# A graph-attention layer and an 8-head attention layer: the fourth pair's product between its scores, the projection and statistics one stretch sooner, the norms later

## The chip, the cores and the metric

The kernel runs on one core of a Trainium2 chip. The metric is the device time of one execution in microseconds (us). Five engines work side by side, each through its own queue in order: TensorE (PE, with PEld for its weight loads), VectorE (DVE), ScalarE (ACT), GpSimd (POOL) and SyncE (SP, which here only issues transfers). Each of them waits for the others through semaphores.

## The reference

The input x has 32 batch entries of 512 nodes with 512 features, and one adjacency matrix of 512 x 512 serves them all. Layer 0 is a graph attention whose output goes beside its own projection; layer 1 is an 8-head attention with heads of 64. Each layer is added to its input and normalised.

```python
# layer 0, per batch entry: W is 512 x 256, a is 2 x 256
h = X @ W
e = leaky_relu(h @ a[0] + (h @ a[1]).T, 0.2) - 1e9 * (1 - adj)
x = layernorm(X + concatenate([softmax(e) @ h, h], axis=-1))
# layer 1, per batch entry and head
q, k, v = (split_heads(x @ W.T + b) for W, b in ((Wq, bq), (Wk, bk), (Wv, bv)))
s = where(adj == 0, -inf, q @ k.T / 8)
x = layernorm(x + merge_heads(softmax(s) @ v) @ Wo.T + bo)
```

All arithmetic is in 32-bit floats.

## The kernel before

A batch entry (below: a batch) is four tiles of 128 nodes. The loop goes over the 32 batches, and in each over four pairs of heads, hp = 0 to 3 (first to fourth pair). Batches 1 to 29 are written by `middle_batch`; the first and the last two by the general loop behind it, with the same steps in a slightly different order. The program is not reordered by any scheduler: each engine executes its instructions in the order in which the Python code emits them. So a step that stands earlier in the code stands earlier in the queue of every engine that it uses, and an instruction that waits holds up all that follows on its engine.

The work of three batches is interleaved. While layer 1's attention of batch b runs, layer 0 of batches b+1 and b+2 and the output projection of batch b-1 fill the gaps. The steps that matter here:

- `head_scores(b, hp, i)` makes the scores of tile i for both heads of a pair on TensorE (L701, into PSUM tiles ps, of which there are four). VectorE adds the mask and takes the row's minimum of the negated scores (L315), and ScalarE takes exponentials (L710) into a tile p.
- `head_blocks` transposes four such tiles p in blocks of 32 x 32 on VectorE into one buffer t (L330). It is called twice a pair, after tiles 0 and 1 and, from `pair_ends`, after tiles 2 and 3.
- `head_move` moves t to the buffer pt by 16 transfers on SP's queue (L347), which finishes the transpose. There is one buffer t and one buffer pt: the next pair's blocks wait until t has been moved away, and the next move waits until pt has been used.
- `head_products` multiplies pt by the values on TensorE (L763, pav), for the pair before the current one (`last`). `head_divide` multiplies the result by the inverse sums on VectorE (L778).
- `project_two(b, s)` makes queries and keys of two pairs with seven products in place of eight (L547, PSUM tiles pw). Three products go to three PSUM banks; ScalarE copies each out (L571: p1, p5, p7, later u2), and the next product adds into the first bank, so that it has to wait for the copy p1. VectorE adds the pieces (L584). `next(two)` runs it up to and with u2.
- `finish_seven(b - 1)` is the output projection of the batch before (L802, pf), with additions to the residual x on VectorE and GpSimd (L825).
- `out_stats(b - 1)` takes mean and variance of the four finished tiles on VectorE (L280, L281); `ln_root` takes the square root on ScalarE (L286), which needs another table of functions than the exponential; `out_norm` takes the reciprocal and shift on VectorE (L291, L911) and normalises on ScalarE (L915); `store` writes the batch out.
- `l0_project(b + 2, i)` is layer 0's projection (L264, ph; copied by ScalarE in L369), `l0_columns` sends the attention terms through DRAM on SP's queue (L387 to L391), `l0_maxima`, `l0_write` and `l0_read` make the row maxima from them (L404, L315, L421, L426).

PSUM tiles of tag m (pav, pf, ph, pw and others) take turns in four banks, in the order of the code. Tiles p, the copies of `project_two` and those of `l0_maxima` take turns in nine buffers.

Of the kernel before, what the change touches and what calls it, by code (L numbers as in the profile page):

```python
# [26 lines left out]
def kernel(  # L27
# [48 lines left out]
    B, N, F = x.shape  # L76
# [3 lines left out]
    NB = N // P  # L80
# [202 lines left out]
    def ln_root(key, tiles=range(NB)):  # L283
        mv, rstd = st["ln", key]
        lo, hi = tiles[0], tiles[-1] + 1
        nc.scalar.activation(rstd[:, lo:hi], mv[:, lo:hi, 1], AF.Sqrt, bias=eps)  # L286
# [84 lines left out]
    def l0_project(b, i):  # L371

        l0_copy(b, i, l0_product(b, i))
# [526 lines left out]
    def out_stats(b):  # L900
        z, key = st["x1", b], f"1_{b}"
        for i in range(NB):
            ln_stats(z, key, i)
# [28 lines left out]
    def steps(todo):  # L932
        for _ in todo:
            pass
# [37 lines left out]
    two = project_two(0, 0)  # L972
# [29 lines left out]
    def middle_batch(b):  # L1002


        seven = finish_seven(b - 1, lambda: load_x(b + 1, nc.gpsimd))
        for hp in range(NP):
            last = (b, hp - 1) if hp > 0 else (b - 1, NP - 1)
            head_scores(b, hp, 0)
            head_scores(b, hp, 1)
            if hp in (1, 2):  # L1010
                head_products(*last)
            if hp == 0:
                values = project_v(b)
                next(values)
                l0_scores(b + 1, [0, 1])
            elif hp == 1:
                next(seven)
                l0_add_h(b + 1)
            elif hp == 2:
                add_bias(b + 1)  # L1020
            head_blocks(b, hp)
            if hp == 3:
                out_stats(b - 1)
                for i in range(NB):
                    l0_project(b + 2, i)
                l0_columns(b + 2)
                ln_root(f"1_{b - 1}")
            head_scores(b, hp, 2)
            head_scores(b, hp, 3)
            if hp == 2:  # L1030
                next(seven)
            else:
                if hp == 3:
                    out_norm(b - 1)
                if hp != 1:
                    head_products(*last)
            pair_ends(b, hp)
            if hp == 2:
                next(seven)
            head_divide(*last)  # L1040
            if hp == 0:
                l0_row(b + 1)
                l0_scores(b + 1, [2, 3])
                leaky(st["row", b + 1])
                next(values)
                l0_weights(b + 1)
                head_inverse(b, 0)
                steps(values)
                next(seven)
                next(seven)  # L1050
            elif hp == 1:
                l0_output(b + 1)
                load_xt(b + 2)
                two = project_two(b, 1)
                next(two)
                l0_norm(b + 1)
                next(two)
                head_inverse(b, 1)
                blocks = x1_blocks(b + 1)
                for part in (blocks, two, blocks, two, blocks):  # L1060
                    next(part, None)
            elif hp == 2:
                steps(seven)
                x1_sums(b + 1, nc.gpsimd)
                head_inverse(b, 2)
                if b == 1:
                    add_bias(1)
            else:
                l0_maxima(b + 2)
                l0_write(b + 2)  # L1070
                l0_read(b + 2)
                store(b - 1)
                steps(project_two(b + 1, 0))
                head_inverse(b, 3)

    before = None
# [1 line left out]
    for b in range(B):  # L1078
        if 0 < b < B - 2:
            middle_batch(b)  # L1080
            before = (b, NP - 1)
            continue
        more = b < B - 1
        seven = finish_seven(b - 1) if b > 0 else None
        for hp in range(NP):

            head_scores(b, hp, 0)
            head_scores(b, hp, 1)  # L1090
            if hp == 0:
                values = project_v(b)
                next(values)
                if more:
                    l0_scores(b + 1, [0, 1])
            elif hp == 1:
                if b == 0:
                    l0_output(1)
                else:
                    if more:  # L1100
                        l0_weights(b + 1)
                        l0_add_h(b + 1)
                    next(seven)
            elif hp == 2:
                if b > 0:
                    next(seven)
                if b > 0 and more:
                    add_bias(b + 1)
            else:
                if b > 0:  # L1110
                    if b + 2 >= B:
                        steps(seven)
                    if not more:
                        output_weights()
                    out_stats(b - 1)
                else:
                    weight_sums(OUTPUT, nc.gpsimd)
                    add_bias(0)
                if b + 2 < B:
                    for i in range(NB):  # L1120
                        l0_project(b + 2, i)
                    l0_columns(b + 2)
                if b > 0 and b + 2 < B:
                    ln_root(f"1_{b - 1}")
            head_scores(b, hp, 2)
            head_scores(b, hp, 3)
            if b > 0 and hp in (1, 2):
                next(seven)
            if b > 0 and hp == 3 and b + 2 < B:
                out_norm(b - 1)  # L1130
            if (b, hp) not in turned:
                head_blocks(b, hp)
                head_reciprocal(b, hp)
                head_sums(b, hp)
                head_move(b, hp)
            if hp == 0 and b > 0 and more:
                load_x(b + 1)
            if before is not None:
                head_values(*before)
            if (b, hp) == (B - 1, 3):  # L1140
                last_products(b, 0)
                last_products(b, 1)
            if (b, hp) in turned:
                head_turn(b, hp)
            if hp == 0:
                if more:
                    l0_row(b + 1)
                    leaky(st["row", b + 1])
                next(values)
                head_inverse(b, 0)  # L1150
                if more:
                    l0_scores(b + 1, [2, 3])
                steps(values)
                if b == 0:
                    l0_weights(1)
            elif hp == 1:
                head_inverse(b, 1)
                if b > 0 and more:
                    next(seven)
                    l0_output(b + 1)  # L1160
                if b + 2 < B:
                    load_xt(b + 2)
                two = project_two(b, 1)
                next(two)
                if more:
                    l0_norm(b + 1)
                next(two)
                blocks = x1_blocks(b + 1) if more else None
                for part in (blocks, two, blocks, two, blocks):
                    if part:  # L1170
                        next(part, None)
                if not more:
                    next(seven)
            elif hp == 2:
                if b == 0:
                    output_bias()
                else:
                    next(seven)
                    if b + 2 < B:
                        steps(seven)  # L1180
                head_inverse(b, 2)
                if more:
                    x1_sums(b + 1, nc.gpsimd)
            else:
                if b + 2 < B:
                    l0_maxima(b + 2)
                    l0_write(b + 2)
                    l0_read(b + 2)
                if b > 0 and b + 2 < B:
                    store(b - 1)  # L1190
                if more:
                    two = project_two(b + 1, 0)
                    next(two)
                    if b + 2 >= B:
                        ln_root(f"1_{b - 1}")
                        out_norm(b - 1)
                        store(b - 1)
                    steps(two)
                head_inverse(b, 3)
                if b == 0:  # L1200
                    weight_negative(OUTPUT)
            before = (b, hp)
    b = B - 1
# [73 lines left out]
```

## Time and profile before

| what | value |
|---|---|
| runs before | 3148.51, 3152.12, 3158.78 us; median 3152.12 us |
| the profiled execution's own time | 3155.16 us |
| its span, first to last instruction | 3153.4 us |
| mean granted TensorE clock | 0.993 |
| TensorE, matmuls busy | 3062.0 us (97%) |
| VectorE busy | 2551.2 us (81%) |
| ScalarE busy | 1535.9 us (49%) |
| GpSimd busy | 1286.3 us (41%) |
| scores L701 on TensorE | 2048 matmuls, 510.0 us |
| product with the values L763 | 2048 matmuls, 469.2 us |
| layer 0's projection L264 | 1024 matmuls, 234.9 us |
| statistics L280 on VectorE | 252, 170.7 us, 677 ns each |
| moves pt<-t on SP's queue | 1984 transfers of 128 KB, 2.4 us each to landing |

How to read it: the busy time of an engine is a sum over the whole span, and neighbouring matmuls overlap, so that 97% does not say that TensorE works at its peak. In the lists of groups the idle time before a group stands beside what ended it. A timeline row has the start in us from the span's start, the time that the row takes, the engine, the line, the operation, the tile written and read, and in square brackets the idle time just before it with the instruction that ended it. One batch takes about 96 us, so a row at 1474.14 lies in the middle of the run, in the fourth pair of a middle batch.

### The profile page before, as it was taken

How to read it: one execution, taken by the hardware profiler on the slowest of the kernel's cores; microseconds unless marked ns; L12 is line 12 of the kernel's file. 1: busy time of each engine (PE TensorE's matmuls, PEld its weight loads, DVE VectorE, ACT ScalarE, POOL GpSimd, SP SyncE). 2: the span in 40 equal slices, each digit the busy share in tenths (PEclk: the TensorE clock that was granted, in tenths of full speed). 3: DMA queues.
4: the chain of work that ended last, by engine and by line, in shares of the span. 5: the costliest groups of instructions: out<-in, count | busy, mean ns of one | idle time of the engine just before them, and what ended most of it. 6: DMA issues, size and time to landing. Idle time of an engine off the chain costs nothing.

```text
span 3153.4 us, 44630 instructions
## 1 busy us (share of the span) xinstructions
PE 3062.0 (97%) x13492; PEld 2072.1 (66%) x13492; DVE 2551.2 (81%) x5707; ACT 1535.9 (49%) x3264; POOL 1286.3 (41%) x1253
## 2 busy tenths in 40 slices
PE   8999999999999999999999999999999999999998
PEld 6666666666666666666666666666666666666665
DVE  7788888788788887888887878888888888788765
ACT  4444455445454444554455544555444555445544
POOL 4354343343434434434434334344344443343421
PEclk9999999999999999999999999999999999999999
DMA  6466656566566666666665656665666656566632
GB/s 185 107 147 160 149 141 160 144 151 152 146 151 143 152 156 146 155 146 145 163 152 141 156 142 154 153 155 146 150 144 164 151 144 159 140 156 151 152 94 64
DMA packets 237440, 462.53 MB, mean 147 GB/s; under 512 B 94544, under 2 KB 97104, under 8 KB 237200
## 3 DMA queue, kind: packets, MB, share of 16 engines
q1 hardware_dynamic: 216848, 395.42, 53.0%
q0 software_dynamic: 20352, 64.25, 6.5%
q8 instruction: 109, 1.79, 0.3%
q14 instruction: 131, 1.07, 0.1%
HBM read 132.65 MB, written 34.27 MB: 53 GB/s over the span
## 4 chain that ended last, share of the span: by engine, by line
PE 66%; DVE 13%; ACT 6%; SPq 6%; issue 4%; DMA 3%; POOL 2%; DVEq 0%; ACTq 0%; POOLq 0%
PE pw L547 18%; PE pv L623 12%; PE ps L701 10%; PE pav L763 9%; PE pf L802 8%; PE po L477 7%; SPq L347 6%; DVE t L330 5%; DVE stats L280 2%; ACT p L710 2%; DVE p L315 2%; ACT x L915 2%; DMA d_tot<-tot 1%; DMA xt<-in_xt_dram 1%; PE ph L264 1%
## 5 line engine op out<-in xcount | busy, mean ns | idle before, releaser
L710 ACT ACTIVATE p<-p,least 128x512 f32<-128x512 f32 x1024 | 726.4, 711 | 681.0 <-DVE least L315 673.5
L330 DVE STREAM_TRANSPOSE t<-p 128x512 f32<-128x512 f32 x992 | 636.3, 686 | 127.1 <-DMA d_tot<-tot 81.0
L315 DVE CUSTOM_DVE_ANT_0 p<-ps,mask 128x512 f32<-128x512 f32 x1024 | 642.0, 682 | 60.7 <-PE ps L701 60.6
L701 PE MATMUL ps<-qk 64*128 64x512 f32 x2048 | 510.0, 615 | 0.3 <-DVE least L315 0.3
L763 PE MATMUL pav<-pt,v 128*64 128x512 f32 x2048 | 469.2, 600 | 2.8 <-DMA pt<-t 2.8
L754 POOL DMA_DIRECT2D inv<-d_tot x256 | 134.1, 528 | 717.0 <-DVE least L315 241.5
L763 PEld LDWEIGHTS pav<-pt,v 128*64 128x64 f32 x2048 | 136.1, 137 | 320.2 <-issue 293.7
L701 PEld LDWEIGHTS ps<-qk 64*128 64x128 f32 x2048 | 177.0, 186 | 235.1 <-issue 153.0
L600 POOL TENSOR_TENSOR p<-p,p 128x512 f32<-128x512 f32 x64 | 83.7, 1308 | 436.0 <-ACT p L571 436.0
L825 POOL TENSOR_TENSOR x<-x,u_o 128x512 f32<-128x512 f32 x93 | 115.6, 1270 | 340.2 <-ACT u_o L820 340.2
L825 DVE TENSOR_TENSOR x<-x,pf 128x512 f32<-128x512 f32 x186 | 125.4, 677 | 150.9 <-POOL x L825 90.8
L477 PE MATMUL po<-h,et 128*128 128x257 f32 x1024 | 236.3, 388 | 2.8 <-ACT et L470 2.2
L264 PE MATMUL ph<-w_sb,xt 128*128 128x258 f32 x1024 | 234.9, 387 | 0.3 <-DVE w_sb L190 0.3
L477 PEld LDWEIGHTS po<-h,et 128*128 128x128 f32 x1024 | 190.6, 191 | 59.7 <-issue 14.2
L264 PEld LDWEIGHTS ph<-w_sb,xt 128*128 128x128 f32 x1024 | 193.3, 191 | 51.3 <-PE ps L701 22.0
L459 POOL TENSOR_TENSOR et<-et,mask0t 128x512 f32<-128x512 f32 x126 | 157.4, 1262 | 121.6 <-ACT et L455 121.5
L547 PE MATMUL pw<-tx,wqx_sb 128*128 128x256 f32 x512 | 138.2, 393 | 68.6 <-ACT p L571 68.6
L710 ACT ACTIVATION_READ_ACCUMULATOR p<-p,least 128x1 f32 x1024 | 192.1, 188 | 0.0
L280 DVE BATCH_NORM_STATS2 stats<-x 128x6 f32<-128x512 f32 x252 | 170.7, 677 | 17.9 <-POOL x L825 4.8
L710 ACT ACT_TABLE_LOAD x62 | 79.5, 1283 | 209.9 <-DVE least L315 209.4
L802 PE MATMUL pf<-wo_sb,ot 128*128 128x256 f32 x744 | 179.4, 384 | 0.0
L286 ACT ACTIVATE rstd<-mv,eps 128x4 f32<-128x4 f32 (+1 forms) x66 | 19.6, 297 | 324.8 <-DVE mv L281 321.7
(155 smaller groups left out, 5608.1 us busy)
## 6 DMA issues: line engine op xcount, KB each, us to landing
pt<-t SPq DMA_DIRECT2D x1984, 128.0 KB, 2.4
inv<-d_tot POOLq DMA_DIRECT2D x256, 128.0 KB, 3.4
xt<-in_xt_dram SPq DMA_DIRECT2D x31, 1024.0 KB, 7.4
x1t<-x1t_b SPq DMA_DIRECT2D x496, 64.0 KB, 2.0
out_dram<-x SPq DMA_DIRECT2D x31, 1024.0 KB, 7.1
x<-in_x_dram POOLq DMA_DIRECT2D x29, 1024.0 KB, 5.6
rows<-d_att SPq DMA_DIRECT2D x31, 512.0 KB, 3.8
rows<-d_least SPq DMA_DIRECT2D x31, 256.0 KB, 4.3
```

The source lines that it names most:

```text
L264: nc.tensor.matmul(ps, lhs(c), rhs(c), start=(c == 0), stop=(c == FC - 1))
L280: nc.vector.bn_stats(stats, z[:, i, :])
L315: nc.vector.tensor_tensor_reduce(out=out, in0=scores, in1=mask, scale=-1.0, scalar=MIN_INIT, op0=ALU.add, op1=ALU.min, accum_out=least,)
L330: nc.vector.transpose(t[:, :, :, i, :].rearrange("p r c q -> p c r q"), src.rearrange("p (c r k) -> p c r k", r=4, k=G),)
L477: nc.tensor.matmul(po, et[:, j, i * P : (i + 1) * P], h_sb[:, j, 2:], start=(j == 0), stop=(j == NB - 1),)
L547: nc.tensor.matmul(ps[:, k * half : (k + 1) * half], weights(k, c), moving(c), start=start and k == 0 and c == 0, stop=c == FC // 2 - 1, s ...
L623: nc.tensor.matmul(ps[:, k * half : (k + 1) * half], columns(k, c), weights(c), start=start and k == 0 and c == 0, stop=c == FC // 2 - 1, ...
L701: nc.tensor.matmul(ps, qk[rows, 0, i * P : (i + 1) * P], qk[rows, 1, :], start=True, stop=True)
L710: nc.scalar.activation(p, p, AF.Exp, bias=least, scale=-1.0, accum_out=total[:, j, i : i + 1])
L763: nc.tensor.matmul(po[j * D : (j + 1) * D, :], st["v", b, c // 2][:, c % 2, head * D : (head + 1) * D], pt[:, :, j, c, :, :].rearrange("p ...
L802: nc.tensor.matmul(ps[:, k * half : (k + 1) * half], columns[:, c, k * P : (k + 1) * P], weights(c), start=start and k == 0 and c == 0, st ...
L825: engine.tensor_tensor(to, to, term.rearrange("p (k d) -> p k d", k=2), ALU.add)
```

## The change

In `middle_batch`, three steps of the fourth pair move:

- the product with the values of the third pair goes from behind the fourth pair's scores to between them: it follows the scores of tiles 0 and 1, as it already did in the second and third pair;
- layer 0's projection of batch b+2 with its attention columns, and the statistics and square root of the finished batch b-1, go from the middle of the fourth pair to the end of the third;
- the norms of batch b-1 go from ahead of the projection of the next queries and keys to behind its first part (behind the copies p1, p5, p7 and u2 on ScalarE).

In the general loop the batch before the last takes its statistics at the same late place as its square root and norms, and no longer in the middle of the fourth pair. No instruction is added or taken away.

```diff
@@ middle_batch
             head_scores(b, hp, 0)
             head_scores(b, hp, 1)
-            if hp in (1, 2):
+            if hp > 0:
                 head_products(*last)
...
             head_blocks(b, hp)
-            if hp == 3:
-                out_stats(b - 1)
-                for i in range(NB):
-                    l0_project(b + 2, i)
-                l0_columns(b + 2)
-                ln_root(f"1_{b - 1}")
             head_scores(b, hp, 2)
             head_scores(b, hp, 3)
             if hp == 2:
                 next(seven)
-            else:
-                if hp == 3:
-                    out_norm(b - 1)
-                if hp != 1:
-                    head_products(*last)
+            elif hp == 0:
+                head_products(*last)
             pair_ends(b, hp)
...
             elif hp == 2:
                 steps(seven)
+                for i in range(NB):
+                    l0_project(b + 2, i)
+                l0_columns(b + 2)
                 x1_sums(b + 1, nc.gpsimd)
                 head_inverse(b, 2)
                 if b == 1:
                     add_bias(1)
+                out_stats(b - 1)
+                ln_root(f"1_{b - 1}")
             else:
                 l0_maxima(b + 2)
                 l0_write(b + 2)
                 l0_read(b + 2)
+                two = project_two(b + 1, 0)
+                next(two)
+                out_norm(b - 1)
                 store(b - 1)
-                steps(project_two(b + 1, 0))
+                steps(two)
                 head_inverse(b, 3)
@@ the general loop
                     if not more:
                         output_weights()
-                    out_stats(b - 1)
+                        out_stats(b - 1)
...
                     next(two)
-                    if b + 2 >= B:
+                    if b == B - 2:
+                        out_stats(b - 1)
                         ln_root(f"1_{b - 1}")
                         out_norm(b - 1)
                         store(b - 1)
```

## The prediction

> **What bounds the kernel now.** I read the page first, then the list of waits, then the timeline of one batch engine by engine, and went back to the other batches for the one wait that counts. The page's busy times and its chain:
>
> ```profile
> PE 3062.0 (97%) x13492; PEld 2072.1 (66%) x13492; DVE 2551.2 (81%) x5707; ACT 1535.9 (49%) x3264; POOL 1286.3 (41%) x1253
> ...
> PE 66%; DVE 13%; ACT 6%; SPq 6%; issue 4%; DMA 3%; POOL 2%; DVEq 0%; ACTq 0%; POOLq 0%
> ```
>
> TensorE looks full, so a gain can only come from its few idle microseconds. Of its idle time the list of waits holds one large entry (total us, times, longest):
>
> ```profile
> PE pw L547 <- ACT p L571: 68.6, 30, 3.3
> ```
>
> It comes once a batch. TensorE from the end of the third pair to the projection of the next batch (start, us):
>
> ```profile
> 1470.40 1.89 PE L802 MATMUL pf<-wo_sb,ot 128*128 128x256 f32 x8
> 1472.22 1.99 PE L701 MATMUL ps<-qk 64*128 64x512 f32 x8
> 1474.14 7.24 PE L264 MATMUL ph<-w_sb,xt 128*128 128x258 f32 x32
> 1481.31 1.99 PE L701 MATMUL ps<-qk 64*128 64x512 f32 x8
> 1483.23 3.65 PE L763 MATMUL pav<-pt,v 128*64 128x512 f32 x16
> 1486.81 1.13 PE L547 MATMUL pw<-x1t,wq_sb 128*128 128x256 f32 x4
> ...
> 1491.23 1.03 PE L547 MATMUL pw<-tx,wk_sb 128*128 128x256 f32 x4
> 1494.51 1.10 PE L547 MATMUL pw<-tx,wqx_sb 128*128 128x256 f32 x4 [2.25 <-ACT p L571]
> ```
>
> Everything else follows back to back. The product at 1494.51 adds into the bank of the first product, which ScalarE must first have copied out (p1). Why that copy is late stands on VectorE and ScalarE:
>
> ```profile
> 1480.83 2.49 DVE L330 STREAM_TRANSPOSE t<-p 128x512 f32<-128x512 f32 x4 [3.87 <-DMA d_tot<-tot]
> ...
> 1486.41 0.66 DVE L315 CUSTOM_DVE_ANT_0 p<-ps,mask 128x512 f32<-128x512 f32 x1
> ```
> ```profile
> 1488.14 0.72 ACT L710 ACTIVATE p<-p,least 128x512 f32<-128x512 f32 x1
> ...
> 1490.98 2.91 ACT L915 ACTIVATE x<-x,shift,rstd 128x512 f32<-128x512 f32 x4
> 1493.80 1.52 ACT L571 COPY p<-pw 128x512 f32<-128x512 f32 x3
> ```
>
> VectorE's transposes wait until buffer t has been moved away, 3.24 us of statistics follow (1483.25 to 1486.41), then the last scores' minima, their exponentials, 2.82 us of norms, and only then p1. The move of t is 16 DMAs one after another on SP's queue:
>
> ```profile
> 1468.55 10.04 SPq L347 DMA_DIRECT2D pt<-t  x16
> ...
> 1492.55 10.13 SPq L347 DMA_DIRECT2D pt<-t  x16
> ```
>
> Some of the stalls cost more than their idle time. In the batch with the wait of 2.65 the next matmuls run at half pace:
>
> ```profile
> 621.47 1.10 PE L547 MATMUL pw<-tx,wqx_sb 128*128 128x256 f32 x4 [2.65 <-ACT p L571]
> 622.41 1.80 PE L547 MATMUL pw<-tx,wkx_sb 128*128 128x256 f32 x4
> 624.00 1.91 PE L547 MATMUL pw<-tx,wq_sb 128*128 128x256 f32 x4
> ```
>
> **What the stall is worth.** From 1472.22 on, the order has no other gap, so the pitch of batches tells it. The projection (L264) starts at 1474.14, 1570.27 and 1665.54: pitches 96.13 and 95.27. The lost time is the step from 1491.23 to 1494.51 less 0.94, the same step where nothing waits (1447.71 to 1448.65): 2.34, and 1.48 in the next batch (1587.36 to 1589.78). Both pitches give a floor of 93.79. The first middle batch has its projection at 214.51 and the 29th at 2921.26, so 2706.75 less 28 x 93.79 = 80.6 were lost, and the 29th loses 2.8 more: 83.4 us. Of this, 15.2 is the slow clock: nine batches of the 29 need 8.83 instead of 7.14 for the rest of the projection, after steps that lost 2.5 to 3.5.
>
> [...]
>
> **The change, part by part**, in the batch at 1474. I put TensorE's new order on the old durations.
>
> *The projection ahead of the fourth pair's scores.* The 32 matmuls start at 1472.22 and end at 1479.39; scores 1479.39 to 1481.31; the product with the values 1481.31 to 1484.89 (3.58); scores to 1486.81; the three first products to 1492.17. No matmul is added. Its four PSUM banks are those of the third pair's output; the last is freed by the addition of 1473.83 to 1474.5, and is needed at 1475.8. Cost nothing, cover 1.3.
>
> *Statistics sooner.* 4 x (0.59 + 0.20) = 3.2 us of VectorE move ahead of the fourth pair's first minima, into idle time: they start at 1474.5; tiles 2 and 3 wait for GpSimd's last addition (ends 1476.39), and the last is done at 1478.0. Queued behind are the minima, which can't start before 1480.6, 1.16 after their scores (as 1501.58 to 1502.74). So hidden, with 2.6 spare. On ScalarE the projection's last copy ends at 1479.85, the attention columns at 1480.1, the load of the square root's table 1481.4, the root 1481.7, the reload for the exponential 1483.0. First exponential at 1483.0. Before, this reload sat between the two halves.
>
> *From there as in the third pair*, whose first exponential at 1459.32 has the second minima 3.59 later, second exponentials at 4.36, all done at 7.3, second transposes done at 8.42. So the fourth pair: minima 1486.6 (the scores are ready at 1486.0), exponentials done 1490.3, p1 out of its bank by 1490.9. Needed at 1492.17: 1.2 spare, and the stall goes. The product of 3.58 that gave the exponentials time between scores and projection is gone as cover; this spare is what is left. The wait for t no longer counts: t is free at 1480.9 (1482 in the slowest batch), the transposes can't start before 1483.9.
>
> *Norms later.* 2.82 us of ScalarE go behind the four copies, about 1496 to 1499; the next exponentials are due at 1501. The reciprocal and shift (0.17 + 0.31) stand ahead of the projection's additions on VectorE, which end at 1498; scores need them at 1499.24. The store waits in SP's queue behind the read of the minima in any case (issued 1506.74). Nothing.
>
> *SP and GpSimd.* SP's write and read of the attention columns come 1.9 sooner, in a gap between the move ending 1478.6 and the next from 1491.5. GpSimd has the 0.12 memset ahead of the four sums for x1 instead of behind; they end at 1481.7 and are read from 1488.5. Nothing.
>
> *What is late next: the moves of t.* TensorE comes 1.92 sooner to the third pair's product, and the moves don't follow. I take a start 0.5 after the last packet's semaphore (rows: waits on the ten semaphores take 1480.44 to 1480.82; elsewhere 0.89 gave no wait, so 0.3 to 0.89). Per batch, from its own issue spans (10.0 to 11.8) and landings (+1.8 mostly):
> - third pair: landings 1.69 to 3.51 ahead of the product, less 1.92, less 0.5: late in 11 of 28 batches, sum 3.5 (1.8 to 8.1);
> - fourth pair: move starts 1491.5 (before 1492.55), product wanted at 1505.0 (before 1507.34): sum 1.1 (0.9 to 2.3);
> - first pair of the next batch: VectorE can't transpose until t is free, 10.0 to 11.5 + 1.85 + 0.4 after 1491.5, that is 1503.8 to 1505.3; its move starts 7.61 later (1505.19 to 1512.80) and takes as long again, against a product at 1524.51: sum 10.0 (8.3 to 11.9).
> Together 14.6 (11.0 to 22.3). If the first exponential comes 1 us later than worked out, 34.5 (45 with 0.89); half a microsecond sooner, 6. Each single wait is under the losses that were followed by the slow clock (2.5 and up).
>
> *The batch before the last* stalls 3.12 (3035.87), runs slow for 1.6, and the last batch waits 2.76 for the move of the fourth pair (3053.17) and runs slow for 1.5. There the third statistic waits 4.85 on GpSimd (3030.04) ahead of the last minima. The change puts the statistics behind: minima at 3023.5, p1 in time at 3029.1, the move from 3031 instead of 3039.54. I take 8 of these 9 us (0 to 9.1, as the last batch may wait elsewhere).
>
> **Sum.** The profiled execution took 3155.16 (span 3153.4 and 1.76 around it), 3.04 above the median of the runs shown. 3155.2 - 83.4 - 8 + 14.6 = 3078. Since it is a floor plus new waits, the old stalls' scatter doesn't carry over, and I leave it there.
>
> **Rivals.**
> *The moves become the bound* (0.16): the exponentials come 1 us later, or landings take longer when requests crowd. For it: SP's 16 issues take 10 us whatever TensorE does, and two moves with two rounds of transposes now fill nearly all of the 41.5 us between first exponential and first product. Against: two of three issue spans are at the short end. 30 to 45 us of waits: 3094 to 3109.
> *p1 stays late* (0.05): with first exponentials 2 us later, 0.9 of the stall stays (26 us), and the moves cost some 55: 3145.
> *Slower* (0.07): the new wait on VectorE. The statistics stand at the head of its queue for GpSimd's additions, and behind them minima, exponentials, p1 and the moves. For it: the batch before the last waits 4.85 that way. Against: in the middle batches GpSimd's additions come before the sums for x1, and end at 1476.39. The root's table is ready at 1481.4, so a statistic at 1478.0 has 3.4 spare; p1 and the moves eat the whole gain when the exponentials are 3 us later, so it decides from an addition ending 6.4 late, at 1482.8. A microsecond beyond that, 29 us more: 3180.
>
> **Numbers.** Forecast 0.72 (3064 to 3092), rivals 0.16, 0.05, 0.07. The lower end takes the short waits and whole edge (3068) and the 7 us by which a run lies under this one; the upper the moves' rival: 3060 to 3110. Measurement tells about 0.3% (9 us) from no change: faster 0.91, same 0.02, slower 0.07.
>
> **What would show it.** Right: no wait of L547 for L571 in middle batches, pitch 94 to 94.6, half-pace matmuls gone, VectorE's transposes (L330) waiting for pt in the first pair rather than the fourth, TensorE's L763 waiting 10 to 20 us for pt in all. Wrong: L547 still waiting; statistics (L280) waiting long on GpSimd; L763 waiting over 40 us.

## The result, and the profile after

| | before | changed |
|---|---|---|
| median of 5 runs | 3152.12 us (3142.48 to 3158.78) | 3069.3 us (3067.68 to 3069.96) |
| the profiled execution's own time | 3155.16 us | 3068.30 us |
| its span | 3153.4 us | 3066.5 us |
| mean granted TensorE clock | 0.993 | 0.999 |
| median pitch of the 28 steps from the first to the 29th middle batch | 96.08 us | 93.73 us |

The changed kernel takes 0.9739 of the time before (95% interval 0.972 to 0.9759), 2.6% less. The forecast was 3078 in a range of 3060 to 3110.

First the page of the changed kernel: busy times with their shares of the span, and the shares of the chain that ended last.

```profile
PE 3035.3 (99%) x13492; PEld 2065.8 (67%) x13492; DVE 2567.0 (84%) x5707; ACT 1551.4 (51%) x3264; POOL 1278.9 (42%) x1253
...
PE 85%; DVE 5%; SPq 3%; DMA 3%; issue 2%; ACT 1%; POOL 1%; DVEq 0%; ACTq 0%; POOLq 0%
```

TensorE's busy time fell by 26.7 us, with the same 13492 matmuls: matmuls at half pace (four in 1.80 and 1.91 us behind the wait of 2.65 in the kernel before, 1.03 where nothing was lost) count as busy time too, and they are gone. The chain that ended last now lies on TensorE for 85% instead of 66%; VectorE's share went from 13% to 5% and ScalarE's from 6% to 1%.

The list of waits of TensorE in the changed kernel (total us, times, longest; the entries for the start and the end of the run are left out):

```profile
PE pav L763 <- DVE least L315: 2.5, 2, 1.3
...
PE pv L623 <- DVE ot L778: 1.7, 3, 0.6
PE pav L763 <- DMA pt<-t: 1.6, 1, 1.6
...
PE pf L802 <- DVE v L657: 1.2, 3, 0.8
```

The entry of 68.6 us, L547 waiting for the copies L571, is gone. What is left are many small waits; by place, about half of them are of the product with the values (L763) for the buffer pt. The list spreads these over several names: an instruction that waits for several semaphores is put down to the one that came last in the records, and where that is `least`, d_tot or d_least of a step long done, it was the move. So the sums below are made by place (where on TensorE's timeline a row starts late), not by name.

TensorE in the fourth pair of a middle batch of the changed kernel:

```profile
1526.86 1.89 PE L802 MATMUL pf<-wo_sb,ot 128*128 128x256 f32 x8
1528.59 7.14 PE L264 MATMUL ph<-w_sb,xt 128*128 128x258 f32 x32
1535.65 1.99 PE L701 MATMUL ps<-qk 64*128 64x512 f32 x8
1537.57 3.65 PE L763 MATMUL pav<-pt,v 128*64 128x512 f32 x16
1541.16 1.99 PE L701 MATMUL ps<-qk 64*128 64x512 f32 x8
1543.07 1.13 PE L547 MATMUL pw<-x1t,wq_sb 128*128 128x256 f32 x4
...
1547.49 1.03 PE L547 MATMUL pw<-tx,wk_sb 128*128 128x256 f32 x4
1548.36 1.03 PE L547 MATMUL pw<-tx,wqx_sb 128*128 128x256 f32 x4
```

The order is the new one, no row has a wait in brackets, and the product that needs p1 starts 0.87 after the one before it (1547.49 to 1548.36), where it took 3.28 before. VectorE and ScalarE in the same batch show why p1 is in time:

```profile
1531.30 0.69 DVE L280 BATCH_NORM_STATS2 stats<-x 128x6 f32<-128x512 f32 x1
...
1534.67 0.18 DVE L281 BATCH_NORM_AGGREGATE mv<-stats 128x2 f32<-128x6 f32 x1
1536.81 0.69 DVE L315 CUSTOM_DVE_ANT_0 p<-ps,mask 128x512 f32<-128x512 f32 x1 [1.96 <-PE ps L701]
...
1540.14 2.82 DVE L330 STREAM_TRANSPOSE t<-p 128x512 f32<-128x512 f32 x4 [0.79 <-ACT p L710]
```
```profile
1538.00 1.28 ACT L710 ACT_TABLE_LOAD   x1
1539.29 0.72 ACT L710 ACTIVATE p<-p,least 128x512 f32<-128x512 f32 x1
...
1546.43 1.04 ACT L571 COPY p<-pw 128x512 f32<-128x512 f32 x2
...
1552.66 2.94 ACT L915 ACTIVATE x<-x,shift,rstd 128x512 f32<-128x512 f32 x4 [1.79 <-DVE shift L911]
```

The statistics end at 1534.85 and VectorE then still waits 1.96 for the scores, so they are hidden. The transposes wait for exponentials and no longer for the move of t. The copy p1 starts 3.36 after the first product of its group (1543.07); over all middle batches this is 3.30 on average, and was 7.00 before (5.95 to 8.08). The norms stand behind the copies. On SP's queue the moves of t in two pairs that follow one another are:

```profile
1524.34 10.12 SPq L347 DMA_DIRECT2D pt<-t  x16
...
1547.87 10.04 SPq L347 DMA_DIRECT2D pt<-t  x16
```

### The profile page after: what moved, and what is told of

It is laid out like the page before. It is cut to its first block, busy times and chain, and to the rows that moved or that the text cites. A ratio compares the mean times of both kernels' runs of the same rounds, so it can differ in the third digit from the quotient of the medians.

```text
span 3066.5 us, 44397 instructions
## 1 busy us (share of the span) xinstructions
PE 3035.3 (99%) x13492; PEld 2065.8 (67%) x13492; DVE 2567.0 (84%) x5707; ACT 1551.4 (51%) x3264; POOL 1278.9 (42%) x1253
## 4 chain that ended last, share of the span: by engine, by line
PE 85%; DVE 5%; SPq 3%; DMA 3%; issue 2%; ACT 1%; POOL 1%; DVEq 0%; ACTq 0%; POOLq 0%
PE pw L547 22%; PE ps L701 13%; PE pav L763 13%; PE pf L802 12%; PE pv L623 10%; PE po L477 7%; PE ph L264 7%; SPq L347 3%; DVE t L330 2%; DVE p L315 1%; DMA inv<-d_tot 1%; ACT p L710 1%; DMA d_tot<-tot 1%; PE pt L741 0%; DMA adjs_sb<-in_adj_dram 0%
## 5 line engine op out<-in xcount | busy, mean ns | idle before, releaser
L763 PE MATMUL pav<-pt,v 128*64 128x512 f32 x2048 | 467.7, 598 | 7.1 <-DVE least L315 2.5
L754 POOL DMA_DIRECT2D inv<-d_tot x256 | 134.1, 528 | 791.2 <-DVE least L315 229.0
L763 PEld LDWEIGHTS pav<-pt,v 128*64 128x64 f32 x2048 | 139.2, 136 | 321.1 <-issue 285.6
L825 POOL TENSOR_TENSOR x<-x,u_o 128x512 f32<-128x512 f32 x93 | 115.6, 1271 | 336.3 <-ACT u_o L820 336.2
L825 DVE TENSOR_TENSOR x<-x,pf 128x512 f32<-128x512 f32 x186 | 125.5, 677 | 138.2 <-POOL x L825 90.8
L264 PE MATMUL ph<-w_sb,xt 128*128 128x258 f32 x1024 | 230.7, 382 | 0.3 <-DVE w_sb L190 0.3
L264 PEld LDWEIGHTS ph<-w_sb,xt 128*128 128x128 f32 x1024 | 194.9, 191 | 30.5 <-issue 0.8
L802 PE MATMUL pf<-wo_sb,ot 128*128 128x256 f32 x744 | 180.2, 385 | 1.2 <-DVE v L657 1.2
L802 PE MATMUL pf<-wox_sb,ot 128*128 128x256 f32 x744 | 176.9, 382 | 0.0
L459 POOL TENSOR_TENSOR et<-et,mask0t 128x512 f32<-128x512 f32 x126 | 150.0, 1212 | 49.3 <-ACT et L455 48.8
L802 PEld LDWEIGHTS pf<-wo_sb,ot 128*128 128x128 f32 x744 | 137.5, 190 | 47.6 <-issue 25.0
```

The costliest lines, as they stand in the source:

```text
L264: nc.tensor.matmul(ps, lhs(c), rhs(c), start=(c == 0), stop=(c == FC - 1))
L763: nc.tensor.matmul(po[j * D : (j + 1) * D, :], st["v", b, c // 2][:, c % 2, head * D : (head + 1) * D], pt[:, :, j, c, :, :].rearrange("p ...
L802: nc.tensor.matmul(ps[:, k * half : (k + 1) * half], columns[:, c, k * P : (k + 1) * P], weights(c), start=start and k == 0 and c == 0, st ...
L825: engine.tensor_tensor(to, to, term.rearrange("p (k d) -> p k d", k=2), ALU.add)
```

## Where the 87 us come from

All terms are against the profiled execution: 3155.16 to 3068.30 is 86.9 us less.

- **The stall at p1** and the half-pace spells after it: 83.4 us, gone in all 29 middle batches.
- **A shorter floor.** A batch without waits takes 93.45 (the shortest pitch measured), not the 93.79 that the prediction worked out from the kernel before, where every batch stalls and the shortest pitch is 95.09. Over 29 batches this is 9.9 us.
- **New waits.** The projection of the first middle batch starts at 212.52 and that of the 29th at 2841.91, a mean pitch of 93.91 over 28 steps (93.45 to 94.81). Less 93.45, times 28: 12.9 us.
- **The batch before the last and the last:** about 6.4 us less, as what is left of the sum. An experiment below gives 5.8.

-83.4 - 9.9 + 12.9 - 6.4 = -86.8.

## The experiments

My theory was that the late copy p1 is the whole matter, that each moved part makes it sooner by its share, and that the moves of t then cost a little. The rivals were that one part alone does it (the norms, or the new order on TensorE), and that the moves set the pace now. The kernel before was run again beside every group of kernels, with medians of 3151.75 to 3153.05, and the changed kernel beside one. All intervals are 95%.

### One part alone: the norms later

The kernel before with one edit, the norms behind the copies in the middle batches:

```diff
-                if hp == 3:
-                    out_norm(b - 1)
...
-                store(b - 1)
-                steps(project_two(b + 1, 0))
+                two = project_two(b + 1, 0)
+                next(two)
+                out_norm(b - 1)
+                store(b - 1)
+                steps(two)
```

> The kernel before with one edit: in the middle batches the norms stand behind the copies p1, p5, p7 and u2. Theory (the copy p1 comes late by what stands ahead of it on ScalarE, and the moves of t are the next limit): the 2.82 us of norms go from ahead of p1, so of the 29 losses only what exceeds 2.82 stays, about 2 us in all, and no half-pace spells. But the fourth pair's move starts 1.06 later against TensorE than in the changed kernel, so waits for pt of about 36 us instead of 14.5 by the same working; the old order's switches cost 0.27 a batch more (8 us); the batch before the last stays as it was (7 us). 3107, between 3095 and 3120. Rival (p1 is late because VectorE waits for t, and the norms only fill time in which ScalarE would wait): the stall of L547 for L571 stays above 40 us, 3135 to 3152.

Measured: 3082.55 us, ratio 0.9776 (0.9761 to 0.979). This one edit brings 70 of the 83 us, far more than I expected, and the time lies below my range. Its list of waits of TensorE:

```profile
PE pw L547 <- ACT p L571: 3.6, 3, 3.1
```

The stall is gone from the middle batches with the norms alone (the longest wait, 3.1, lies in the batch before the last); p1 starts 4.08 after the first product (7.00 before, 3.30 in the changed kernel). I had put the moves 1.06 us later than in the changed kernel, and they come only 0.25 later (4.99 against 4.74 after the first product). What I left out: the reciprocal and shift, which belong to the norms, stood on VectorE ahead of the second transposes (1488.83 to 1490.0 in the batch of the prediction) and went away with them. In the kernel before:

```profile
1488.83 0.17 DVE L291 RECIPROCAL rstd<-rstd 128x4 f32<-128x4 f32 x1
1489.04 1.04 DVE L911 SCALAR_TENSOR_TENSOR shift<-mv,rstd 128x4 f32<-128x4 f32 x1
1490.00 2.48 DVE L330 STREAM_TRANSPOSE t<-p 128x512 f32<-128x512 f32 x4
```

So the waits are not the 36 us expected but 18.0: mean pitch 94.28 over a shortest of 93.64, times 28.

The shortest pitch also splits the missed term of the floor: 93.79 worked out for the kernel before, 93.64 measured here, 93.45 in the changed kernel. About 0.15 goes with the wait for p1 and 0.19 with the new order on TensorE.

The whole change is 15.8 us faster than this (3066.77 on another chip): 10.4 from the pitch (0.37 x 28) and about 5 from the end, which this kernel has as before (4.9 to 5.8 by the experiment on the end below).

### All but the norms

The changed kernel with the norms ahead of the projection again:

```diff
+            elif hp == 3:
+                out_norm(b - 1)
...
-                two = project_two(b + 1, 0)
-                next(two)
-                out_norm(b - 1)
                 store(b - 1)
-                steps(two)
+                steps(project_two(b + 1, 0))
```

> The changed kernel with the norms of the middle batches ahead of the projection again. Theory: p1 comes 2.82 later and has 1.2 spare, so TensorE loses 1.6 a batch at p1, 47 us, no half-pace spells; TensorE then comes later to the products, so most of the 13 us of waits for pt go. 3100 to 3112. Rival (the sooner statistics and the product's place alone end the stall): 3069 to 3075.

Measured: 3104.35 us, ratio 0.9847 (0.9832 to 0.9862), as expected.

```profile
PE pw L547 <- ACT p L571: 41.1, 32, 1.4
```

The other parts alone bring 49 us. Here p1 starts 6.13 after the first product: still late, but only by so much that each loss is at most 1.4, and no half-pace matmuls follow (the granted clock is 0.999). The norms alone bring 70 and the rest alone 49, together they bring 83 to 86: both act on the same lateness, and what either brings depends on whether the other is there.

### The statistics back between the scores

The changed kernel with statistics and root between the two halves of the fourth pair, as before, and everything else new:

```diff
             head_blocks(b, hp)
+            if hp == 3:
+                out_stats(b - 1)
+                ln_root(f"1_{b - 1}")
...
-                out_stats(b - 1)
-                ln_root(f"1_{b - 1}")
```

> The changed kernel with the statistics and square root of the middle batches back between the halves of the fourth pair; projection, product and norms stay as changed. Theory: the 3.2 us of statistics and the root's two table loads stand between the halves again; the second exponentials start 3 us later than in the changed kernel less what the first gain, p1 is 0.7 late (20 us), the fourth pair's move starts 1.5 later against VectorE, 0.75 against TensorE, some 12 us of waits more: 3095 to 3110. Rival (VectorE has idle time enough in the fourth pair, and the place of the statistics is worth nothing): 3066 to 3072.

Measured: 3134.22 us, ratio 0.9946 (0.9929 to 0.9963). The direction was right, the size was not: of the gain only 19 us are left. The list of waits, and ScalarE in one batch of this kernel:

```profile
PE pw L547 <- ACT p L571: 45.5, 30, 1.6
```
```profile
1475.29 1.28 ACT L286 ACT_TABLE_LOAD   x1
1479.76 0.30 ACT L286 ACTIVATE rstd<-mv,eps 128x4 f32<-128x4 f32 x1 [3.18 <-DVE mv L281]
1480.07 1.28 ACT L710 ACT_TABLE_LOAD   x1
...
1484.20 1.53 ACT L571 COPY p<-pw 128x512 f32<-128x512 f32 x3
```

ScalarE loads the root's table at once and then waits 3.18 for the last statistic, which VectorE ends at 1479.72. The exponentials behind it start at 1481.37 and the first copy at 1484.20, 6.30 after the first product. The projection of 7.17 used to lie between the halves and covered this; in the new order only the product of 3.58 lies there. The loss is 1.8 us a batch at p1 (52 in 29 batches), and the later moves bring the mean pitch to 96.06. The norms stand late here too, and alone they brought 70 us; so the new order on TensorE without the sooner statistics takes back some 50 of them: the sooner projection and the sooner statistics belong together.

### The product with the values last again

The changed kernel with the third pair's product behind all four scores of the fourth, as before:

```diff
-            if hp > 0:
+            if hp in (1, 2):
                 head_products(*last)
...
-            elif hp == 0:
+            elif hp != 1:
                 head_products(*last)
```

> The changed kernel with the product with the values behind the fourth pair's four scores. Theory (the product between the scores gives VectorE time to free the four banks of scores): the scores of tile 3 wait until the minima of tile 1 are done, 0.9 us a batch, 26 us; p1 comes no later, and TensorE's lateness takes about 10 us of the waits for pt away. 3080 to 3090, with TensorE's L701 waiting for VectorE's L315. Rival 1 (the place of the product is worth nothing): 3066 to 3072. Rival 2 (the product is needed as cover for the exponentials ahead of p1): L547 waits for L571, over 3095.

Measured: 3084.59 us, ratio 0.9784 (0.977 to 0.9799), as expected. TensorE in one batch:

```profile
1447.10 4.87 PE L701 MATMUL ps<-qk 64*128 64x512 f32 x16
1451.90 3.65 PE L763 MATMUL pav<-pt,v 128*64 128x512 f32 x16
```

The sixteen score matmuls take 4.80 in one run, where two runs of eight take 2 x 1.92: the second eight wait for VectorE to empty the four PSUM tiles ps of the first. The wait stands at their weight loads (PEld), four times, 1.7 us of idle time in all:

```profile
1449.02 0.29 PEld L701 LDWEIGHTS ps<-qk 64*128 64x128 f32 x2 [0.76 <-DVE least L315]
```

This is 0.96 a batch; the pitch is 94.41 and nearly constant, 0.96 over the floor of 93.45. p1 starts even sooner (2.39 after the first product) and the waits for pt are nearly gone, so 28 us are paid and some 13 saved. The product between the scores is thus not what removes the stall. It fills time in which the scores would wait.

### The end of the run as before

The changed kernel with the general loop's old place of the statistics in the batch before the last:

```diff
                     if not more:
                         output_weights()
-                        out_stats(b - 1)
+                    out_stats(b - 1)
...
-                    if b == B - 2:
-                        out_stats(b - 1)
```

> The changed kernel with the general loop as before: the batch before the last takes its statistics in the middle of the fourth pair again. Theory: the stall at p1 (3.1), the wait for the move in the last batch (2.8) and their slow spells come back, less the waits that stand there now: 5 to 9 us slower than the changed kernel, 3074 to 3078. Rival (the last batch waits elsewhere for what it gained): within 2 us of the changed kernel.

Measured: 3072.61 us, ratio 0.9744 (0.9731 to 0.9757). The changed kernel ran beside it with

> The changed kernel once more, beside the three that follow on the same chip: 3067 to 3071.

and took 3066.77 us (3063.16 to 3072.1), ratio 0.9727 (0.9712 to 0.9743). The edge is worth 5.8 by the medians; from the last projection to the end it takes 229.61 against 224.74, so 4.9 by the profiles. The runs of the two overlap by 0.8 us, so the size is good to a few microseconds only.

### What the delay of the moves costs, and a surprise

To see how steep the price of later moves is, the small write of the sums (d_tot) went ahead of the sixteen moves on SP's queue, in `pair_ends` and for all pairs of the middle batches:

```diff
+            head_sums(b, hp)
             head_move(b, hp)
-            head_sums(b, hp)
```

> The changed kernel with the write of the sums of exponentials (d_tot) ahead of the 16 moves of each pair on SP's queue, in the middle batches: every move starts 0.65 us later, nothing else changes. Theory (the moves are the next limit): waits for pt rise from 14.5 to 44 by the same working from the spans and landings of the kernel before, so 29 us slower than the changed kernel, 3098 (3088 to 3108). Rival (what is lost over the shortest pitch has nothing to do with the moves): within 3 us of the changed kernel.

Measured: 3295.48 us, ratio 1.0446 (1.042 to 1.0472): 229 us slower than the changed kernel beside it, where I expected some 30. The waits of TensorE, and the start of the output projection in one batch:

```profile
PE pf L802 <- DVE v L657: 85.4, 29, 3.3
PE pav L763 <- DMA pt<-t: 37.9, 17, 4.8
```
```profile
1582.56 2.79 PE L802 MATMUL pf<-wo_sb,ot 128*128 128x256 f32 x8 [3.07 <-DVE v L657]
```

The new stall is at another place, in the first pair: the projection pf needs PSUM banks that VectorE frees when it adds the values v (L657). After the wait of 3.07 the eight matmuls take 2.79, where the same row of the changed kernel has 1.93: slow matmuls behind a wait, as in the kernel before. VectorE is late because of the four subtractions L469 ahead of v. Here they are in this kernel, with GpSimd beside them:

```profile
1574.38 7.52 DVE L469 TENSOR_TENSOR et<-et,row 128x512 f32<-128x512 f32 x4
```
```profile
1575.32 1.71 POOL L673 TENSOR_TENSOR p_v<-p_v 128x512 f32<-128x512 f32 x1
1576.98 1.05 POOL L754 DMA_DIRECT2D inv<-d_tot  x2
1578.05 1.28 POOL L839 TENSOR_TENSOR to<-ot,ot 128x512 f32<-128x512 f32 x1
...
1580.07 1.28 POOL L842 TENSOR_TENSOR ot<-ot 128x512 f32<-128x512 f32 x1
```

and in the changed kernel:

```profile
1570.99 3.45 DVE L469 TENSOR_TENSOR et<-et,row 128x512 f32<-128x512 f32 x4
```
```profile
1570.36 1.73 POOL L673 TENSOR_TENSOR p_v<-p_v 128x512 f32<-128x512 f32 x1
1579.99 1.04 POOL L754 DMA_DIRECT2D inv<-d_tot  x2 [7.91 <-DVE x L825]
```

The same four instructions take 7.52 us beside a busy GpSimd and 3.45 where GpSimd, after its first addition, stands still until 1579.99. It stands still because its load of the inverse sums (L754) waits for the sums in DRAM, which SP writes only behind the sixteen moves. (The bracket names VectorE's L825, which came last by the records. SP issued the write of the sums at 1577.48, and the load started 2.51 later; the median time of such a write to landing is 2.5.) With the write ahead of the moves the load is ready at once, and GpSimd's additions behind it run into VectorE's subtractions. GpSimd's waits for this write, first in the changed kernel and then in this one:

```profile
POOL inv L754 <- DMA d_tot<-tot: 227.6, 33, 21.3
```
```profile
POOL inv L754 <- DMA d_tot<-tot: 22.4, 2, 21.3
```

So the edit changed two things, and two more kernels take them apart. The first delays the moves by one more small write that nobody reads, and leaves the sums behind:

```diff
+            d = dram.tile([2, P, NB], F32, name=f"d_extra_{b}_{hp}", tag="dextra")
+            nc.sync.dma_start(d.rearrange("j p i -> p j i"), st["tot", b, hp])
             head_move(b, hp)
             head_sums(b, hp)
```

> The changed kernel with one more small write (the sums once more, to a scratch tile that nobody reads) ahead of the 16 moves of each pair on SP's queue, in the middle batches; the write that counts stays behind the moves. So every move starts 0.6 us later, as with the sums ahead, but GpSimd, whose load inv waits for that write, is released no sooner. Theory (the 226 us of the sums ahead came from GpSimd's earlier release, which put its additions beside VectorE's row subtraction L469): L469 stays near 1.05 us, and what is left is the price of later moves, 29 us: 3098, between 3085 and 3115. Rival (0.6 us of delay of the moves alone tips VectorE's chain over): L469 stays near 1.05, but TensorE's L802 waits for L657 and the time is over 3200.

Measured: 3092.62 us, ratio 0.9811 (0.9798 to 0.9825), as expected; the mean pitch is 94.83. The delay of the moves alone costs about 26 us against the changed kernel's 3066.77 (on another chip). The second puts the sums ahead in the first pair alone, where L469 stands:

```diff
+            if hp == 0:
+                head_sums(b, hp)
             head_move(b, hp)
-            head_sums(b, hp)
+            if hp > 0:
+                head_sums(b, hp)
```

> The changed kernel with the write of the sums ahead of the moves in the first pair alone, in the middle batches. The fourth pair's moves start as in the changed kernel; GpSimd's load inv of the first pair no longer waits until the moves are issued, so its next additions (L839, L842) run beside VectorE's row subtraction. Theory (the two engines slow each other): L469 takes 1.6 us or more each instead of 1.05, v is late, TensorE's L802 waits for L657 some 1 to 3 us a batch: 3110 to 3200. Rival (the later moves of the fourth pair were the cause): L469 as before, under 3085.

Measured: 3257.8 us, ratio 1.033 (1.0315 to 1.0345), 191 us slower than the changed kernel and above my range. The group of L469 (count, busy us, mean ns) in the changed kernel, and then with the first pair's sums ahead:

```profile
L469 DVE TENSOR_TENSOR et<-et,row 128x512 f32<-128x512 f32 x124 | 119.3, 1020 | 1.0
```
```profile
L469 DVE TENSOR_TENSOR et<-et,row 128x512 f32<-128x512 f32 x124 | 210.3, 1753 | 1.0
```

With the extra write the mean is 1061 ns, so there VectorE is hardly touched. The waits of TensorE with the first pair's sums ahead:

```profile
PE pf L802 <- DVE v L657: 76.7, 29, 4.0
PE pav L763 <- DMA pt<-t: 40.8, 17, 3.9
```

This settles that the early release of GpSimd in the first pair makes nearly all of the loss, and that the delay of the moves does not. From 1020 to 1753 ns, times 124, VectorE has 91 us more. Of the 191 us, 76.7 are waits at pf and 40.8 waits for the moves. The granted clock is 0.979 against 0.999; 2% of 3258 us would be 65 us, an estimate. TensorE's busy time for the same matmuls says the same: 3102.2 us against 3034.9 in the changed kernel run again, 67 more. That the clock falls because of the waits, and not by itself, is argued from the slow rows behind the waits.

### Fewer moves on SP's queue

If the new waits come from the sixteen moves in a row on SP's queue, sharing them out should take most of the 12.9 us back. In the fourth pair of the middle batches, GpSimd issues four of the sixteen; its copy pn, which would stand in front, goes ahead of them:

```diff
-    def move_pair(dst, t):
+    def move_pair(dst, t, shared=False):
...
-                nc.sync.dma_start(
+                engine = nc.gpsimd if shared and r == 3 else nc.sync
+                engine.dma_start(
...
-        move_pair(pt, st.pop(("t", b, hp)))
+        move_pair(pt, st.pop(("t", b, hp)), 0 < b < B - 2 and hp == 3)
...
+            elif hp == 3:
+                l0_pn(b + 2)
             pair_ends(b, hp)
```

(`l0_pn` is the copy pn, taken out of `l0_maxima`.)

> The changed kernel with 4 of the 16 moves of the fourth pair issued by GpSimd, in the middle batches; the copy pn stands ahead of them on GpSimd. Theory: SP is done 2.5 us sooner, the fourth pair's and the next first pair's products no longer wait, 11 us of waits go: 3058 (3055 to 3062), the shortest pitch as before and the mean near it. Rival (transfers issued by GpSimd start late or land late, as its loads inv take 3.4 to landing against 2.4): as the changed kernel or slower, 3067 to 3085.

Measured: 3058.84 us (3058.03 to 3059.48), ratio 0.9701 (0.9688 to 0.9714), as expected. What is left of the waits for pt in its list (where the product with the values is line 769):

```profile
PE pav L769 <- DMA pt<-t: 1.0, 1, 1.0
```

The mean pitch is 93.60 over a shortest of 93.44: 4.6 us of waits in 28 steps. The changed kernel on the same chip has 10.8 (93.83 over 93.45). That is 6.1 us less; the profiled executions of the two differ by 6.3 (3064.28 and 3058.03), the medians by 7.9. The new place of the copy pn was not run by itself. This version is faster than both kernels; the ranges of its runs and of the changed kernel's do not touch, though a quarter of a per cent is near the limit of what can be told. The same for the third pair too (`hp >= 2` in place of `hp == 3`):

> As the kernel with 4 of 16 moves of the fourth pair on GpSimd, and 4 of 16 of the third pair too, where GpSimd waits some 11 us for ScalarE. Theory: the waits for pt of the third pair go, 3 us: 3056 (3053 to 3059). Rival (the additions of the output projection that follow on GpSimd come later and hold up the statistics): 3062 or more.

Measured: 3059.18 us (3056.38 to 3060.21), ratio 0.9702 (0.9688 to 0.9715): no gain over the fourth pair alone, and just above the range I gave. The mean pitch is 93.70. The third pair's waits were worth 1.6 us in all, so there was little to take: they are gone, but 3.8 us of waits stand at the first pair's product, where the version with the fourth pair alone has none. A second buffer t, so that VectorE need not wait for the moves, was not tried.

## Why the prediction was right, step by step

- **The stall of 83.4 us goes.** Right. There is no wait of L547 for L571 in the middle batches, and the half-pace matmuls are gone with it: the granted clock is 0.999. By the starts of the rows, the prediction's spells of 8.83 against 7.14 are 8.76 against 7.07, and the losses of 2.5 to 3.5 ahead of them are 2.49 to 3.43; the price of a spell, 1.69, and the sum stay as they are.
- **The projection ahead costs nothing; cover 1.3.** Right: L264 follows pf without a gap (1526.86 to 1528.59).
- **The statistics are hidden.** Right. With TensorE's offset between the two batches (1472.22 to 1528.59, 56.37), they were to end at 1534.4 and ended at 1534.85; the first exponential was to start at 1539.4 and started at 1539.29; the copy p1 at 1546.7, measured 1546.43; the fourth pair's move at 1547.87, measured 1547.87. With the statistics back between the scores the loss was 1.8 a batch at p1, so this step carries much of the gain.
- **The norms later cost nothing.** Right, and they are the largest single part: alone they bring 70 us. The prediction priced the edits together and did not say which of them was enough.
- **The floor of 93.79** failed. "No matmul is added" was right, but the same matmuls in another order are 0.34 us a batch shorter, 9.9 us in all. From start to start, the order before has pf 1.82, ps 1.92, ph 7.17, ps 1.92, pav 3.58, sum 16.41; the new one pf 1.73, ph 7.06, ps 1.92, pav 3.59, ps 1.91, sum 16.21. The rows write the size of the weights behind the tiles: pf, ph and pw have 128*128, the scores 64*128, the product with the values 128*64. Before, TensorE left the full-size products twice (pf to ps, ph to ps) and came back twice (ps to ph, pav to pw); now, with pf and ph side by side, once each. So 0.20 goes with one way out and back; that the size of the weights is the reason is read from these rows, and no run changed it alone. The other 0.14 is the start-up after a wait, which I had left in the floor: the step to the product that needs p1 takes 0.87 and not the 0.94 that I deducted, and the products from there to the next scores take 7.00 instead of 7.07. This is the largest error of the sum: of the 10 us between the sum (3078.4) and the profiled 3068.3 the floor makes 9.9, the new waits make 1.7, and the edge takes 1.6 back.
- **The new waits of 14.6** came out at 12.9, but partly at other places. Third pair's product: predicted 3.5, measured 1.6 (5 times). Fourth pair's: 1.1 and 1.2. Next first pair's: 10.0 and 3.8 (6 times). Another 6.2 us stand at two places that I had counted at nothing, both in the first pair: the values' products (L623) waiting for VectorE's division L778, 3.4 with the start-up behind it, and the output projection (L802) waiting for v, 2.8. There VectorE is late, because its transposes wait for t. Its list of waits in the changed kernel has:

```profile
DVE t L330 <- DMA d_least<-least: 20.4, 13, 2.7
DVE t L330 <- DMA d_tot<-tot: 11.4, 8, 2.2
```

  The transfers named are the small ones that SP issues just behind a move, and the rows with these waits lie in the first pair, as predicted. Before, the same transposes waited 81.0 and 24.2, in the fourth. The mechanism (moves that don't follow TensorE) was right; I followed it on SP's queue up to the product, and not on VectorE through the rest of the first pair. That the sum of 14.6 came so near to 12.9 is in part luck: TensorE loses 10.0 in the first pair as predicted, but 6.2 of it ahead of the product. So two of the signs that I gave were not met: the mean pitch is 93.91, just under 94 to 94.6, and L763 waits 6.6 us for pt in all and not 10 to 20.
- **The edge of 8** came out at 5 to 6.4, within its bounds (0 to 9.1).
- **The rivals.** The moves became no bound: the delay by one more small write shows how near it was, with 26 us for about half a microsecond a pair (such a write takes 0.36 to 0.53 on SP's queue, 1.76 once). p1 stayed late in two of the kernels with one part undone, and there the times were about as large as the losses at p1 and the waits for the moves say. The statistics waited for GpSimd 2.9 us in all, at most 0.2 at a time, inside VectorE's spare time.
- **The slow clock.** In the kernel before, the granted clock is 0.81 in the spell from 621.47 to 630.23, and 1.00 in the one from 1398.38 to 1405.46, of the usual length. The nine slow spells of the middle batches follow losses of 2.49 to 3.43, but four other batches lost 2.60 to 2.99 and had none, so the size of the loss alone does not tell where one follows. In the kernel with the sums ahead, slow rows follow a loss of 3.07 as well. What else decides it was not shown.

## What to carry to other kernels

Where a wait comes once a batch, look at everything that stands between its cause and the instruction that ends it, on all engines; a step that is small on its own engine (the norms with their reciprocal and shift, 70 of the 83 us) can be enough. Parts of a change that act on the same lateness don't add up (70 and 49 us alone, 83 to 86 together), and a part that takes away another's cover must be made together with it. A wait that costs nothing where it stands can keep an engine out of another's way (GpSimd's for the sums in the first pair, 191 us): before a wait is removed, look at what the released engine will do next, and beside whom.

## What the runs showed of the hardware

- **VectorE beside GpSimd.** A subtraction L469 of two 128x512 tensors takes 0.68 us (one starts every 0.60) with GpSimd standing still, 81 times of 124 in the changed kernel, and 1.53 to 1.76 us beside GpSimd's additions L459 and L673 (42 times; 2.51 once). With the sums ahead in all pairs its mean is 1.87 us, with the first pair's ahead 1.75. What it costs is seen in the two kernels that released GpSimd early, 229 and 191 us. Why VectorE is slower there was not shown: no run changed the kind of work that GpSimd has beside L469.
- **Order of TensorE's products.** Leaving products with weights of 128*128 for the scores of 64*128 costs 0.09 us (pf 1.82 before the change, 1.73 after it), and coming back 0.11 (ph 7.17 and 7.06).
- **Sixteen score matmuls in a row** cost 0.96 more than two runs of eight (4.80 against 2 x 1.92): their weight loads wait four times, 1.7 us in all, for VectorE to empty the four PSUM tiles.
